# Attention scores by 32-row strips of the array instead of one masked 128-row product

## Chip, core and metric

The kernel runs on one core of a Trainium2 chip. The metric is the device time of one execution in microseconds (us). All data is float32. Engines are named as in the profile: PE is the matrix engine (PEld its weight loads), DVE the vector engine, ACT the scalar engine, POOL GpSimd, SP the engine that issues most DMAs. A "record" is one line of the profiler's own log: each float32 matmul leaves two weight-load records and two matmul records, each transpose by the identity one of each.

## What is computed

Four residual layers on x of shape (16, 256, 128), each on a layernorm of x:

```python
x = x + attn_a(ln(x))   # softmax in blocks of 64 tokens, 16 heads of 8
x = x + ffn(ln(x))      # top 2 of 8 experts, hidden 512, silu(g) * u
x = x + attn_b(ln(x))   # attention over the FIRST axis (16 positions), plus a bias
x = x + ffn(ln(x))      # same experts and weights

def attn_a(x):                       # b, block n, token i/j, head h, d = 8
    scores = einsum('bnihd,bnjhd->bnhij', q, k) / sqrt(8)
    return einsum('bnhij,bnjhd->bnihd', softmax(scores), v)
def attn_b(x):                       # sequence of 16, one per t of 256; same heads
    scores = einsum('bhqd,bhkd->bhqk', q / sqrt(8), k) + bias
    return einsum('bhqk,bhkd->bqhd', softmax(scores), v) @ out_w.T + out_b
```

## The kernel before

**Data and stages.** x lies in SBUF as four quarters `xq[q]` of 64 tokens, each 128 partitions by 8 groups by 128 channels. A group is two sequences of 64 tokens, so attention A has 32 groups of two blocks. Attention B has 32 groups of 128 tokens too, taken two at a time ("dg", 16 of them). Each quarter of attention is followed by `router`, which sorts token rows by expert into DRAM; `experts` then runs units of 256 or 128 rows.

**Order of work.** The main loop (L1199 to L1250) weaves generators: each `yield` is a step, and `weave` spreads steps of the router, of the next `prepare_a` or `begin_b` and of expert units between the steps of `attention_a` or `attention_b`. The counts BEGIN_A and BEGIN_B (L1190) tell `weave` how many steps a side has. From that the tile framework's scheduler makes one fixed order per engine when the kernel is built; each engine runs its order strictly in sequence and waits on semaphores. PSUM buffers are few: two for scores (`ps_sc`), two for all transposes, values and outputs (`ps_mm`, tag mm), three for `ps_gu`.

**Queries and keys.** `prepare_a` and `prepare_b` make, for half a quarter (512 tokens), the transposed q and k with channels on partitions: partition 32r + 8j + d holds head 4r + j, channel d. `keys` (L410) writes four copies of k by four ACT instructions in `four` (L388, recorded at L391); copy j keeps only the channels of the heads with index j in each strip of 32 partitions and is zero elsewhere (mask K_HM). `queries` (L404) also writes four copies: copy r keeps only the strip of partitions 32r to 32r + 31 (`q_scale`, `q_bias`, built at L371 to L380).

**Scores.** With those zeros a full 128-row product gives the right heads. In `attention_a` (L473), for each block b of a group, two matmuls (L487) with 128 stationary columns (two copies r by 64 tokens) and 256 moving columns (four copies j by 64 tokens) fill the bank `sc` of that block. In `attention_b` (L563), four matmuls per group (L593) with 128 stationary columns (four copies r by 32 tokens) and 128 moving ones fill one bank.

**After the scores.** In A, DVE takes the row maxima `mx` (L495) and writes sc - mx to `ex` (L496), ACT takes the exponential (L500), PE transposes `ex` (L506, `t_A`), ACT copies that to `eT` (L510), and 16 small matmuls with 64 stationary columns (L517, `o_A`) make the output, which `divided` (L442) normalises. B is the same with the bias added first (L600, `sb`) and outputs from 16 matmuls of 32 stationary columns (L630, `o_B`).

Of the kernel before, what the change touches and what calls it, by code (L numbers as in the profile page):

```python
# [114 lines left out]
def hybrid_kernel(  # L115
# [169 lines left out]
    def psum(name):  # L285
        return ps_mm.tile([P, 512], F32, tag="mm", name=name)
# [80 lines left out]
        nc.gpsimd.tensor_tensor(xs, xs, row.unsqueeze(1).to_broadcast([P, 4, C]), ALU.add)  # L367

    q_scale = const.tile([P, 4], F32, name="q_scale")  # L371
    q_bias, k_bias = {}, {}
    for r in range(4):
        nc.vector.tensor_reduce(
            q_scale[:, r : r + 1], k_sb[:, K_ID + 32 * r : K_ID + 32 * (r + 1)], AX.X, ALU.max
        )
    nc.vector.tensor_scalar(q_scale, q_scale, SCALE, None, ALU.mult)
    for col in (B_Q, B_IQ):
        q_bias[col] = const.tile([P, 4], F32, name=f"q_bias{col}")
        nc.vector.tensor_scalar(q_bias[col], q_scale, b_sb[:, col : col + 1], None, ALU.mult)  # L380
    for col in (B_K, B_IK):
        k_bias[col] = const.tile([P, 4], F32, name=f"k_bias{col}")
        nc.vector.tensor_scalar(
# [15 lines left out]
    def product(src, w, name):  # L399
        p = ps_gu.tile([P, CH], F32, tag="gu", name=name)  # L400
        nc.tensor.matmul(p, lhsT=w, rhs=src, start=True, stop=True)
        return p

    def queries(qT, src, w, col, name):  # L404
        yield from four(
            lambda r, p: (qT[:, :, r, :], p.rearrange("p (a k) -> p a k", k=qT.shape[3])),
            product(src, w, f"q_{name}"), q_scale, q_bias[col],
        )

    def keys(kx, src, w, col, name):  # L410
        yield from four(
# [47 lines left out]
    def prepare_a(q, half):  # L459
        n = f"A{q}_{half}"  # L460
        lnT = p2.tile([P, CH // BS, 2, BS], F32, tag="src", name=f"lnT_{n}")
        qT = p2.tile([P, CH // BS, 4, BS], F32, tag="qT", name=f"q_{n}")
        kx = p2.tile([P, 4, CH], F32, tag="kx", name=f"k_{n}")

        def put(_, pt):
            nc.scalar.copy(*spread(lnT, pt, 2))

        yield from layernorm_t(q, [half], n, put)
        yield from keys(kx, lnT[:, :, 0], wk_sb, B_K, n)
        ready[q, half] = lnT, qT, kx  # L470
        yield from queries(qT, lnT[:, :, 0], wq_sb, B_Q, n)

    def attention_a(q, half):  # L473
        lnT, qT, kx = ready.pop((q, half))
        for g in range(4 * half, 4 * half + 4):
            n = f"A{q}_{g}"
            vt = va[g % 2]
            values(vt, lnT, g % 4, 2, wv_sb, n)
            yield


            ex = p2.tile([P, 2, 8, BS], F32, tag="ex", name=f"ex_{n}")
            for b in range(2):
                sc = ps_sc.tile([P, 512], F32, tag="sc", name=f"sc_{n}_{b}")
                blk = 2 * (g % 4) + b
                for v in range(2):
                    nc.tensor.matmul(  # L487
                        sc[:, v * 4 * BS : (v + 1) * 4 * BS],
                        lhsT=qT[:, blk, 2 * v : 2 * v + 2, :].rearrange("p r k -> p (r k)"),
                        rhs=kx[:, :, blk * BS : (blk + 1) * BS],  # L490
                        start=True, stop=True,
                    )
                sc3 = sc.rearrange("p (h k) -> p h k", k=BS)
                mx = p3.tile([P, 16], F32, tag="mx", name=f"mx_{n}_{b}")
                nc.vector.tensor_reduce(mx[:, 0:8], sc3, AX.X, ALU.max)  # L495
                beat[0] = nc.vector.tensor_tensor(  # L496
                    ex[:, b], sc3, mx[:, 0:8].unsqueeze(2).to_broadcast([P, 8, BS]),
                    ALU.subtract,
                ).ins
                turn_of[0] = nc.scalar.activation(ex[:, b], ex[:, b], AF.Exp).ins  # L500
                yield
            eT = p2.tile([P, 2, 4, P], F32, tag="eT", name=f"eT_{n}")
            for b in range(2):
                pt = psum(f"t_{n}_{b}")
                for i in range(4):
                    nc.tensor.transpose(  # L506
                        pt[:, i * P : (i + 1) * P],
                        ex[:, b, 2 * i : 2 * i + 2, :].rearrange("p h k -> p (h k)"), ident,
                    )
                turn_of[0] = nc.scalar.copy(eT[:, b].rearrange("p a b -> p (a b)"), pt).ins  # L510
                yield
            po = psum(f"o_{n}")
            for b in range(2):
                for i in range(8):

                    u, v = i // 2 % 2, i // 4
                    nc.tensor.matmul(  # L517
                        po[b * BS : (b + 1) * BS, i * 18 : (i + 1) * 18],
                        lhsT=eT[:, b, 2 * v + i % 2, u * BS : (u + 1) * BS],
                        rhs=vt[:, b, 2 * i : 2 * i + 2, :].rearrange("p h d -> p (h d)"),  # L520
                        start=True, stop=True,
                    )
            att = divided(po[:, 0 : H * (D + 1)], n)
            beat[0] = att_last[0]
            if g == 4 * half:
                add_row(q, half, bv_bc)
            nc.gpsimd.tensor_tensor(xq[q][:, g, :], xq[q][:, g, :], att, ALU.add)  # L527
            yield
# [15 lines left out]
    def prepare_b(q, half):  # L544
        n = f"B{q}_{half}"
        xt = p2.tile([P, CH // 32, 4, 32], F32, tag="src", name=f"xt_{n}")
        qT = p2.tile([P, CH // 32, 4, 32], F32, tag="qT", name=f"q_{n}")
        kx = p2.tile([P, 4, CH], F32, tag="kx", name=f"k_{n}")
        px = psum(f"xt_{n}")
        nc.tensor.matmul(  # L550
            px, lhsT=wt_sb, rhs=ready[q][:, half * CH : (half + 1) * CH], start=True, stop=True
        )
        nc.scalar.activation(  # L553
            *spread(xt, px, 4), AF.Identity, bias=b_sb[:, B_TOR : B_TOR + 1]
        )
        yield
        yield from keys(kx, xt[:, :, 0], wi_sb[:, P : 2 * P], B_IK, n)
        ready[q, half] = xt, qT, kx
        yield from queries(qT, xt[:, :, 0], wi_sb[:, 0:P], B_IQ, n)
# [3 lines left out]
    def attention_b(q, half):  # L563
# [15 lines left out]
        for dg in range(2 * half, 2 * half + 2):  # L579
# [3 lines left out]
                yield  # L583


            ex = p2.tile([P, 2, H, 32], F32, tag="ex", name=f"ex_B{q}_{dg}")
            for gg in range(2):
                g = 2 * dg + gg
                n = f"B{q}_{dg}_{gg}"
                sc = ps_sc.tile([P, 512], F32, tag="sc", name=f"sc_{n}")  # L590
                for j in range(4):
                    blk = 4 * (g % 4) + j
                    nc.tensor.matmul(  # L593
                        sc[:, j * P : (j + 1) * P],
                        lhsT=qT[:, blk].rearrange("p r k -> p (r k)"),
                        rhs=kx[:, :, blk * 32 : (blk + 1) * 32],
                        start=True, stop=True,
                    )
                sb = p2.tile([P, H, 32], F32, tag="sb", name=f"sb_{n}")
                nc.vector.tensor_tensor(  # L600
                    sb, sc.rearrange("p (h k) -> p h k", k=32),
                    pair_bias.unsqueeze(1).to_broadcast([P, H, 32]), ALU.add,
                )
                yield
                mx = p3.tile([P, 16], F32, tag="mx", name=f"mx_{n}")
                nc.vector.tensor_reduce(mx, sb, AX.X, ALU.max)
                beat[0] = nc.vector.tensor_tensor(
                    ex[:, gg], sb, mx.unsqueeze(2).to_broadcast([P, H, 32]), ALU.subtract
                ).ins
                turn_of[0] = nc.scalar.activation(ex[:, gg], ex[:, gg], AF.Exp).ins  # L610
                yield
            for gg in range(2):
# [15 lines left out]
                for j in range(4):  # L628
                    for r in range(4):
                        nc.tensor.matmul(  # L630
                            po[32 * j : 32 * (j + 1), r * 36 : (r + 1) * 36],
                            lhsT=eT[:, 0, j, 32 * r : 32 * (r + 1)],
                            rhs=vb[gg][:, j, 4 * r : 4 * r + 4, :].rearrange(
                                "p h d -> p (h d)"
                            ),
                            start=True, stop=True,
                        )
# [549 lines left out]
        yield from normal_b(q)  # L1187
        yield from prepare_b(q, 0)

    BEGIN_A, BEGIN_B = 3 + 4, 5 + 10 + 5  # L1190
    ALONE = 8

    FIRST = BEGIN[0] + ALONE
# [5 lines left out]
    for layer in range(2):  # L1199
# [10 lines left out]
        for hq in range(2 * NQ):  # L1210
# [15 lines left out]
            else:  # L1226
                main = attention_b(q, half)
                if half == 0:
                    sides.append((prepare_b(q, 1), 5, 0, 3 * n // 4))
                elif q < NQ - 2:  # L1230
                    sides.append((begin_b(q + 1), BEGIN_B, 0, 4 * n // 5))
                wanted, goal = (0, GOAL[hq]) if q < NQ - 1 else (1, OWN[hq])
# [59 lines left out]
```

## Time and profile before

| what | value |
|---|---|
| runs, us | 1013.77 median of 3 (1010.72 to 1017.89) |
| profiled execution, us | 964.67 |
| its span from first to last instruction, us | 962.9 |
| granted PE clock, mean over the span | 0.943 |
| PE busy | 836.8 us (87%) |
| PEld busy | 715.1 us (74%) |
| DVE busy | 554.3 us (58%) |
| ACT busy | 482.1 us (50%) |
| POOL busy | 336.5 us (35%) |
| attention A, scores: first to last matmul | 18.0 to 282.4 us |
| attention B, scores: first to last matmul | 468.4 to 730.8 us |
| score matmul records A, B | 256 of 426 ns, 256 of 285 ns (mean) |

Durations come from the profiled execution, which was about 5% shorter than the runs. The end of a matmul is modelled by the profiler and contains the emptying of the array, so records of neighbouring matmuls overlap; the spacing of starts tells what a matmul costs in a sequence.

### The profile page before, as it was taken

To read this page: it belongs to the slowest core of one execution; us is meant where nothing else is said; L and a number is where in the kernel's file an instruction comes from. 1 tells how busy PE (TensorE), PEld (TensorE's weight loads), DVE (VectorE), ACT (ScalarE), POOL (GpSimd) and SP (SyncE) were. 2 spreads that over 40 slices of the span, in tenths; PEclk is the share of its full clock that TensorE was granted. 3 is DMA by queue.
4 is the path that set the end of the run, shared out by engine and by line. 5 is a ranking of instruction groups with operands and counts; after the bars stand their busy time and mean duration, and the time that the engine had idled before them with its cause. 6 is when DMAs were issued, how large, how long until landed. Compare 5 with 4: busy or idle time off the path is not lost.

```text
span 962.9 us, 18911 instructions
## 1 busy us (share of the span) xinstructions
PE 836.8 (87%) x6684; PEld 715.1 (74%) x6684; DVE 554.3 (58%) x1653; ACT 482.1 (50%) x1029; POOL 336.5 (35%) x381
## 2 busy tenths in 40 slices
PE   4999798979999989996978768996888899899993
PEld 2777676768888779995856656895577787799983
DVE  2666665654856944544673664684369478444563
ACT  4667366357345434444744746742664433344441
POOL 2112360532355563332000162162224537433321
PEclk9999999799999999997997989998999899999997
DMA  7800000043215538995400021317310443699994
GB/s 164 255 20 1 18 29 1 29 140 137 89 65 181 185 99 319 306 325 192 142 23 1 1 79 46 115 47 257 122 45 29 150 144 121 231 326 310 351 386 112
DMA packets 67006, 134.71 MB, mean 140 GB/s; under 512 B 9088, under 2 KB 46720, under 8 KB 66912
## 3 DMA queue, kind: packets, MB, share of 16 engines
q1 hardware_dynamic: 56400, 114.70, 35.9%
q0 software_dynamic: 8640, 17.97, 5.4%
q8 instruction: 53, 0.87, 0.4%
q10 hardware_dynamic: 1872, 0.83, 0.4%
q14 instruction: 41, 0.34, 0.1%
HBM read 112.33 MB, written 27.43 MB: 145 GB/s over the span
## 4 chain that ended last, share of the span: by engine, by line
PE 37%; DVE 9%; ACT 8%; DMA 5%; issue 3%; POOL 1%; SPq 1%; POOLq 0%; DVEq 0%; ACTq 0%
PE u L1057 8%; PE g L1057 8%; PE acc L995 7%; PE v_B L428 3%; DMA xin<-sorted_in 2%; PE o_B L630 2%; PE sc_B L593 2%; DMA w<-w_all 2%; ACT ln_B L345 1%; ACT k_B L391 1%; ACT xt_B L553 1%; PE y L1013 1%; DVE th L1071 1%; DVE h L1073 1%; ACT q_B L391 1%
## 5 line engine op out<-in xcount | busy, mean ns | idle before, releaser
L1023 POOL DMA_INDIRECT results<-yo,to x142 | 139.5, 983 | 259.4 <-ACT yo L1019 225.8
L1071 DVE SCALAR_TENSOR_TENSOR th<-th,g 128x512 f32<-128x512 f32 x142 | 96.8, 681 | 117.0 <-ACT th L1070 116.4
L1057 PE MATMUL u<-xT,w 128*128 128x128 f32 (+1 forms) x864 | 155.5, 318 | 8.0 <-DVE th L1071 7.9
L1057 PE MATMUL g<-xT,w 128*128 128x128 f32 (+1 forms) x864 | 154.7, 315 | 8.4 <-DMA w<-w_all 5.5
L995 PE MATMUL acc<-h,w 128*128 128x128 f32 (+1 forms) x864 | 153.0, 314 | 4.1 <-DVE h L1073 4.1
L780 POOL DMA_INDIRECT sorted_in<-rows,pos_i_F x128 | 124.9, 976 | 79.7 <-issue 28.7
L1070 ACT ACTIVATE th<-g 128x512 f32<-128x512 f32 x142 | 84.9, 598 | 116.0 <-PE g L1057 112.2
L1057 PEld LDWEIGHTS g<-xT,w 128*128 128x128 f32 x864 | 124.2, 194 | 20.4 <-issue 7.2
L1057 PEld LDWEIGHTS u<-xT,w 128*128 128x128 f32 x864 | 124.8, 198 | 17.1 <-DVE th L1071 11.4
L995 PEld LDWEIGHTS acc<-h,w 128*128 128x128 f32 x864 | 123.6, 195 | 12.5 <-DVE h L1073 6.4
L1073 DVE TENSOR_TENSOR h<-th,u 128x512 f32<-128x512 f32 x142 | 97.3, 685 | 16.3 <-PE u L1057 6.7
L487 PE MATMUL sc_A<-k_A,q_A 128*128 128x256 f32 x256 | 78.5, 426 | 18.5 <-DVE ex_A L496 13.8
L517 PEld LDWEIGHTS o_A<-va,eT_A 128*64 128x64 f32 x1024 | 61.1, 141 | 15.5 <-ACT eT_A L510 6.3
L487 PEld LDWEIGHTS sc_A<-k_A,q_A 128*128 128x128 f32 x256 | 47.2, 208 | 29.2 <-issue 8.6
L1003 ACT COPY yT<-acc 128x128 f32<-128x128 f32 (+1 forms) x108 | 32.3, 299 | 69.1 <-PE acc L995 67.8
L517 PE MATMUL o_A<-va,eT_A 128*64 128x18 f32 x1024 | 65.7, 215 | 0.8 <-ACT eT_A L510 0.7
L988 ACT COPY xT<-xt 128x128 f32<-128x128 f32 (+1 forms) x108 | 32.3, 299 | 60.4 <-PE xt L986 57.5
L495 DVE TENSOR_REDUCE mx_A<-sc_A 128x8 f32<-128x512 f32 x64 | 43.4, 679 | 29.0 <-PE sc_A L487 29.0
L510 ACT COPY eT_A<-t_A 128x512 f32<-128x512 f32 x64 | 36.1, 588 | 42.2 <-PE t_A L506 41.9
L1019 ACT ACTIVATE yo<-y,xin 128x128 f32<-128x128 f32 x142 | 48.0, 364 | 13.2 <-PE y L1013 13.2
L527 POOL TENSOR_TENSOR xq<-xq,att_A 128x128 f32<-128x128 f32 x32 | 14.6, 456 | 111.0 <-DVE att_A L447 76.6
L500 ACT ACTIVATE ex_A<-ex_A 128x512 f32<-128x512 f32 x64 | 39.9, 636 | 26.6 <-DVE ex_A L496 26.5
(181 smaller groups left out, 1349.4 us busy)
## 6 DMA issues: line engine op xcount, KB each, us to landing
w<-w_all SPq DMA_DIRECT2D x108, 768.0 KB
back<-results SPq DMA_DIRECT2D x14, 512.0 KB
xin<-sorted_in SPq DMA_DIRECT2D x74, 66.0 KB
xin<-sorted_in SPq DMA_DIRECT2D x34, 132.0 KB
results<-yo,to POOLq DMA_INDIRECT x142, 3.9
w_all<-in_wg SPq DMA_DIRECT2D x1, 2048.0 KB
w_all<-in_wu SPq DMA_DIRECT2D x1, 2048.0 KB
w_all<-in_wd SPq DMA_DIRECT2D x4, 512.0 KB
```

The source lines that it names most:

```text
L487: nc.tensor.matmul(sc[:, v * 4 * BS : (v + 1) * 4 * BS], lhsT=qT[:, blk, 2 * v : 2 * v + 2, :].rearrange("p r k -> p (r k)"), rhs=kx[:, :, ...
L495: nc.vector.tensor_reduce(mx[:, 0:8], sc3, AX.X, ALU.max)
L500: turn_of[0] = nc.scalar.activation(ex[:, b], ex[:, b], AF.Exp).ins
L517: nc.tensor.matmul(po[b * BS : (b + 1) * BS, i * 18 : (i + 1) * 18], lhsT=eT[:, b, 2 * v + i % 2, u * BS : (u + 1) * BS], rhs=vt[:, b, 2 * ...
L780: put_row = nc.gpsimd.indirect_dma_start(out=sorted_in[layer], out_offset=bass.IndirectOffsetOnAxis(ap=pos_i[:, k, g : g + 1], axis=0), in ...
L995: nc.tensor.matmul(acc[:, 0:size], lhsT=w[:, 2, hc * P : (hc + 1) * P], rhs=h[:, j * size : (j + 1) * size], start=(hc == 0), stop=(hc == ...
L1019: nc.scalar.activation(y[:, b, :], py[:, b * P : (b + 1) * P], AF.Identity, scale=t[:, b, C : C + 1],)
L1023: put_row = nc.gpsimd.indirect_dma_start(out=results[layer], out_offset=bass.IndirectOffsetOnAxis(ap=to[:, b : b + 1], axis=0), in_=y[:, b ...
L1057: nc.tensor.matmul(p[:, j * size : (j + 1) * size], lhsT=w[:, k, hc * P : (hc + 1) * P], rhs=xT[:, 0:size], start=True, stop=True,)
L1070: turn_of[0] = nc.scalar.activation(th, pg, AF.Tanh, scale=0.5).ins
L1071: nc.vector.scalar_tensor_tensor(th, th, 1.0, pg, ALU.add, ALU.mult)
L1073: beat[0] = nc.vector.tensor_tensor(h, th, pu, ALU.mult).ins
```

## The change

The query is written once, unmasked, by one ACT instruction: `qT` becomes 128 partitions by 512 tokens. Each score product is split by strip r: stationary operand `qT[32r:32r+32, block]`, moving operand the same 32 partitions of the four key copies. The result of strip r goes to its own output partitions.

- A: eight matmuls per group (32 rows, 64 stationary columns, 256 moving) in place of four. A bank now holds strips 2v and 2v + 1 of both blocks, where it held both halves of one block; the loops after it run over v, and `o_A` picks its operands accordingly. Both banks are allocated ahead of all eight matmuls.
- B: 32 matmuls per pair of groups (32 rows, 32 stationary columns, 128 moving) in place of eight, j outermost, then the group gg, then r. Strip r of group gg lands on output partitions 32((r + gg) mod 4); `o_B` reads it back from there. Both banks are allocated ahead.
- `queries` has one step less, so BEGIN_A, BEGIN_B and the count for `prepare_b` fall by one.

```diff
-    q_scale = const.tile([P, 4], F32, name="q_scale")
     q_bias, k_bias = {}, {}
-    for r in range(4):
-        nc.vector.tensor_reduce(
-            q_scale[:, r : r + 1], k_sb[:, K_ID + 32 * r : K_ID + 32 * (r + 1)], AX.X, ALU.max
-        )
-    nc.vector.tensor_scalar(q_scale, q_scale, SCALE, None, ALU.mult)
     for col in (B_Q, B_IQ):
-        q_bias[col] = const.tile([P, 4], F32, name=f"q_bias{col}")
-        nc.vector.tensor_scalar(q_bias[col], q_scale, b_sb[:, col : col + 1], None, ALU.mult)
+        q_bias[col] = const.tile([P, 1], F32, name=f"q_bias{col}")
+        nc.vector.tensor_scalar(q_bias[col], b_sb[:, col : col + 1], SCALE, None, ALU.mult)
...
     def queries(qT, src, w, col, name):
-        yield from four(
-            lambda r, p: (qT[:, :, r, :], p.rearrange("p (a k) -> p a k", k=qT.shape[3])),
-            product(src, w, f"q_{name}"), q_scale, q_bias[col],
-        )
+        behind_act(
+            nc.scalar.activation(
+                qT, product(src, w, f"q_{name}"), AF.Identity, bias=q_bias[col], scale=SCALE
+            )
+        )
+        yield
...
+            scs = [
+                ps_sc.tile([P, 512], F32, tag="sc", name=f"sc_{n}_{v}") for v in range(2)
+            ]
             for b in range(2):
-                sc = ps_sc.tile([P, 512], F32, tag="sc", name=f"sc_{n}_{b}")
                 blk = 2 * (g % 4) + b
-                for v in range(2):
+                of_blk = slice(blk * BS, (blk + 1) * BS)
+                for r in range(4):
+                    of_r = slice(32 * r, 32 * (r + 1))
                     nc.tensor.matmul(
-                        sc[:, v * 4 * BS : (v + 1) * 4 * BS],
-                        lhsT=qT[:, blk, 2 * v : 2 * v + 2, :].rearrange("p r k -> p (r k)"),
-                        rhs=kx[:, :, blk * BS : (blk + 1) * BS],
-                        start=True, stop=True,
+                        scs[r // 2][
+                            r % 2 * BS : (r % 2 + 1) * BS, b * 4 * BS : (b + 1) * 4 * BS
+                        ],
+                        lhsT=qT[of_r, of_blk], rhs=kx[of_r, :, of_blk], start=True, stop=True,
                     )
...
+            for j in range(4):
+                for gg in range(2):
+                    blk = 4 * ((2 * dg + gg) % 4) + j
+                    of_blk = slice(blk * 32, (blk + 1) * 32)
+                    for r in range(4):
+                        of_r = slice(32 * r, 32 * (r + 1))
+                        to = (r + gg) % 4 * 32
+                        nc.tensor.matmul(
+                            scs[gg][to : to + 32, j * P : (j + 1) * P],
+                            lhsT=qT[of_r, of_blk], rhs=kx[of_r, :, of_blk],
+                            start=True, stop=True,
+                        )
...
-    BEGIN_A, BEGIN_B = 3 + 4, 5 + 10 + 5
+    BEGIN_A, BEGIN_B = 3 + 3, 5 + 10 + 4
```

## The prediction

> **What bounds the kernel now.** I read the busy shares first, then the stages, then the timeline around the scores, then the chain of work that ended last.
>
> ```profile
> PE 836.8 (87%) x6684; PEld 715.1 (74%) x6684; DVE 554.3 (58%) x1653; ACT 482.1 (50%) x1029; POOL 336.5 (35%) x381
> PEclk9999999799999999997997989998999899999997
> ```
>
> PE has the most work at nearly full clock; no other engine is above 58%. Busy time by stage says whether that holds where the change is (columns: stretch, length, then busy PE, PEld, DVE, ACT, POOL with their records, clock, DMA share, GB/s):
>
> ```profile
> 70.00:120.00 50.00, 42.89 (x351) 34.16 (x350) 30.23 (x105) 27.11 (x54) 15.61 (x18) 0.93 0.03 9
> 230.00:292.00 62.00, 60.65 (x454) 51.63 (x453) 40.70 (x126) 26.82 (x55) 26.87 (x31) 0.97 0.22 72
> 475.00:600.00 125.00, 96.78 (x999) 77.67 (x996) 71.60 (x241) 68.96 (x122) 26.69 (x27) 0.88 0.11 33
> ```
>
> Attention A (18 to 292 us) has PE busy for 249 of 274 us over its stretches; attention B (460 to 760) for 250 of 300, and much less at 475 to 600, where it waits. PE's waits at the scores are short: 13.8 us in all for DVE's `ex` (the bank is still being read), 6.8 us for ACT's `q_A`. From 352 us on the chain of waits is complete, and has the four query copies in a row once per quarter:
>
> ```profile
> 464.08 2.11 ACT q_B L391 x3
> 515.87 2.68 ACT q_B L391 x4
> 585.56 2.68 ACT q_B L391 x4
> 696.03 2.11 ACT q_B L391 x3
> ```
>
> So PE's own stream counts in both stages, discounted where it waits, and a shorter query step counts in B.
>
> **The change part by part.**
>
> *1. Price of a score product now.* In a stream PE pays starts, not durations.
>
> ```profile
> 468.38 1.06 PE L593 MATMUL sc_B<-k_B,q_B 128*128 128x128 f32 x8
> 491.86 0.92 PE L630 MATMUL o_B<-vb,eT_B 128*32 128x36 f32 x32 [0.96 <-ACT eT_B L623]
> 492.71 0.55 PE L617 MATMUL t_B<-k_sb,ex_B 128*128 128x128 f32 x3
> 70.06 0.38 PE L487 MATMUL sc_A<-k_A,q_A 128*128 128x256 f32 x1
> 70.37 1.83 PE L517 MATMUL o_A<-va,eT_A 128*64 128x18 f32 x32
> ```
>
> Eight sc_B records take 1.06 us; less the last one's 0.275 that is 0.112 us each, taken below as 0.107 for 128 columns and 0.213 for 256 (proportional to columns). A: 128 matmuls x 2 x 0.213 = 54.7 us. B: 128 x 2 x 0.107 = 27.3 us. Together 82 us.
>
> *2. Do products of different strips run together?* One after the other the new ones cost more: A 256 x 0.427 = 109 us, B 512 x 0.213 = 109 us, 136 us more. The nearest row is `o_B`: its 32 records go to four output strips, eight to each. By proportion 36 columns cost 0.030 us, serially 0.97 us for all; the trace has 32 in 0.92 with a last one of 0.20, so (0.92 - 0.20) / 31 = 0.023 us apart. Single starts tell why: the strips begin at 491.861, 492.019, 492.176 and 492.334, each strip keeps its own pace of 0.032 us, and the second strip starts before records six to eight of the first (492.045, 492.078, 492.110). So strips of output columns do overlap here, and records enter at 0.158 / 8 = 0.020 us, 0.040 per matmul. That is output strips alone; strips of input rows occur nowhere in this trace. The Trainium skill, "TensorE: Matmul & The Clock Gate", Part 3, says they overlap too, but that matmuls start strictly in program order. By that rule the second record of a strip holds up all behind it: in unbroken runs A would take 9 x 0.213 = 1.92 us a group (1.71 before), B 33 x 0.107 = 3.5 us a pair (1.71), together 6.8 + 29 = 36 us more. By the row (starts out of order) it is what follows under 3. I take the row, and keep the rule as a rival.
>
> *3. The order in which they are issued.* The built order of PE's instructions breaks the scores up. Of A's 256 matmuls 26 stand alone, 14 runs have two, 19 three, 13 four, 14 more: 86 runs with other work between. B's 512 stand in 43 runs, seven alone. With 0.040 us per entry and each strip serial (0.427 us a matmul in A, 0.213 in B) I add up each run to its slowest strip: A 55.9 us, B 28.3, together 84.2 against 82.0. The overlap only pays for the split. If every group were one run, A would take 0.97 a group, 31 us.
>
> *4. Changes of tile size.* The last sc_A record starts at 70.06, and streams 0.213; `o_A` starts 0.31 after it, so 0.094 is lost. `o_B` to `t_B` gives 0.129 - 0.032 = 0.097. The built orders hold 156 such changes before and 369 after: 213 more, some 140 in A and 73 in B. At 0.094: 13.2 and 6.9 us.
>
> *5. Lookahead.* Before, the first score bank of an A group was finished ahead of the previous group's first transpose in 27 of 31 cases; after, in 10 of 31, and in 8 not even ahead of its outputs. DVE then starts `mx` and `ex` (0.679 each) later, and behind it wait exp on ACT, the transposes and `o_A`. 17 groups x up to 1.36 = 23 us; below nothing it cannot fall. I take a third, 8 us, since two groups are in flight. In B the first bank is ready after 27 x 0.040 + 0.213 = 1.3 us where it was 0.85: 16 x 0.45 = 7 us, half of it exposed, 3 us.
>
> *6. Query copies.* ACT issues one instruction in place of four, 0.67 us apart (2.68 / 4): 2.0 x 16 = 32 us less on an engine that is busy for half the time. Their writing is contiguous now, which I price as before. On the chain in B stand (0.15 + 2.11) + 2.68 + 2.68 + (2.11 + 0.15) = 9.9 us, and 9.9 - 4 x 0.67 = 7.2 us go. In A `q_A` was waited for 6.8 us; I take 4 off. The setup's DVE instructions go at nothing: DVE waits for the first load of x then, and uncovered they'd be under 2 us.
>
> *Sum.* PE's extra stream is exposed by some 0.6 (between 0.3, if it falls into its waits, and 1). A: (1.3 + 13.2) x 0.6 + 8 - 4 = +12.7. B: (1.0 + 6.9) x 0.6 + 3 - 7.2 = +0.5. Together +13 on 964.7 us. The runs' median is 1.05 times that execution; scaled alike +14, so 1028 us.
>
> Nothing is added for DVE, POOL or the queues: row counts and shapes on DVE stay the same, and SP's transfers keep their order.
>
> **The rivals.**
>
> *ACT's relief decides: faster.* Place: ACT's FIFO, where exponentials and `eT` copies stand behind query copies. For it: the chain rows above, and waits of the outputs on `eT_A` (7.0 us). Against it: ACT is at 50%, and PE's added stream follows the same loop. Price: my sum has 11 of the 32 us come through; the time falls below that of before from 13 + 11 = 24 on; at all 32 the sum is 13 + 11 - 32 = -8, and with the PE stream mostly hidden (exposure 0.3) -15: 999 us.
>
> *Strips overlap only in part.* By the program-order rule +36 us, or, if two row strips cannot write to one bank together (the Trainium skill, "TensorEngine Tiling (Array Packing)", Gotcha 1, unqualified as to partitions; no run here shows it), B's four strips of a bank go in turn: 16 x 3.4 - 27 = +27. With the changes of size, 36 + 20 = 56, exposed by 0.7 (lookahead 11 and relief 11 cancel): about +40, 1055 us. `o_B` speaks against it.
>
> *No overlap of row strips (the change does not do what it says).* +136 + 20 us on PE, 0.75 exposed: +118, 1135 us.
>
> **How the numbers follow.** Small loss 0.47, own range 1008 to 1048; ACT's relief 0.23, 985 to 1006; partial overlap 0.18, 1040 to 1080; none 0.12. From low to high 990 to 1080 leaves out the last and a little of the second. A measurement of this kernel tells about 1% (10 us). Faster by over 1%: 0.22 of the relief's 0.23. Within 1% (1003.6 to 1023.9): 0.19 of the small loss and 0.01 of the relief, 0.20. Slower: 0.28 + 0.18 + 0.12 = 0.58.
>
> **What would show it.** Starts of one strip's records 0.213 us (A) and 0.107 (B) apart with other strips' between them: step 2. About 0.1 us between stream end and next start in 213 new places: step 4. A longer wait of `mx_A` for `sc_A` (29.0 us now): step 5. `q_A` and `q_B` with 16 instructions each and fewer than 3 us on the chain: step 6. The forecast is wrong if the granted clock in 18 to 292 us falls under 0.9, if score records are spaced serially, or if PE waits so long anyway that 20 us of changes vanish.

## The result and the profile after

The changed kernel takes 1108.17 us (median of 4, 1097.42 to 1117.24) against 1013.99 (1010.72 to 1017.89): 1.089 times before, 95% interval 1.080 to 1.098. Ratios and intervals leave out a kernel's slow runs, those over 1.5% above its fastest (here the one of 1117.24). The forecast was 1028 us with a range of 990 to 1080, so it is wrong in size; the direction is right.

The chips on which these kernels ran differ: the kernel before takes 965 to 966 us on some, 1014 to 1023 us on others. Each run's time is therefore given as a ratio to the kernel before on the same chip. Profiles could not be paired like that: the profile of before is from a chip of the first kind (965 us), the first profile of the change from one of the second.

The page of the changed kernel, span, busy shares and granted clock, the rows shown of before:

```profile
span 1095.6 us, 20904 instructions
PE 950.1 (87%) x7708; PEld 748.2 (68%) x7708; DVE 558.9 (51%) x1648; ACT 453.7 (41%) x981; POOL 336.0 (31%) x381
PEclk9557656555688999899979797899799899899997
```

PE's share is 87% as before, ACT has lost the 28 us of query copies, DVE has hardly moved. The third row is new: attention A lies in slices 1 to 15, and in slices 2 to 11 the array gets 5 to 7 tenths of its clock where it had 7 to 9. The busy times per stretch for 200 to 300 us, before and then after (columns: stretch, length, busy PE, PEld, DVE, ACT, POOL with their records, then the clock):

```profile
200.00:300.00 100.00, 94.10 (x680) 79.01 (x679) 60.86 (x201) 49.54 (x103) 39.92 (x47) 0.97 0.35 117
```
```profile
200.00:300.00 100.00, 96.58 (x539) 63.46 (x540) 41.33 (x144) 34.82 (x64) 27.13 (x32) 0.55 0.04 13
```

PE is busy nearly all the time in both, and gets through 539 records where it got through 680; DVE and ACT are busy for about a third less. PE hardly waits; it is slow. Stage A, from the first score record to the last output record, goes from 270.0 to 375.7 us, 106 of the 133 us between the two spans:

```profile
18.00:288.00 270.00, 245.41 (x1960) 199.50 (x1960) 161.98 (x524) 154.32 (x286) 93.44 (x111) 0.95 0.24 75
```
```profile
17.30:393.00 375.70, 353.83 (x2217) 240.76 (x2218) 165.21 (x524) 141.56 (x263) 93.31 (x111) 0.66 0.18 55
```

Length times clock is 258 before (0.954) and 248 after (0.659): counted at full clock, the stage has become no longer. The mean is a share of time, for the profile's clock is either 1 or 0.5. In stage A it fell to half 6 times before and 7 times after; the longest such stretch was 10 us before and is 102 us after:

```profile
182.40:284.70 102.30, 98.71 (x512) 64.80 (x511) 39.95 (x147) 33.12 (x62) 22.30 (x27) 0.50 0.03 8
```

In the chain of waits of the changed kernel PE has 66%, and the score line leads.

```profile
PE 66%; DVE 10%; ACT 7%; issue 6%; DMA 5%; another core or an unknown queue 2%; POOL 2%; SPq 1%; POOLq 0%; DVEq 0%; ACTq 0%
PE sc_A L487 10%; PE g L1067 9%; PE u L1067 9%; PE acc L1005 8%; PE o_A L518 7%; PE t_A L507 4%; PE v_A L423 3%; PE v_B L423 2%; PE o_B L640 2%; PE y L1023 2%; PE lg_F L687 2%; DMA w<-w_all 2%; PE sc_B L600 1%; DMA xin<-sorted_in 1%
```

The strips do run together. The timeline of PE at four products of A in a row (eight records, at half clock), and at one pair of groups of B:

```profile
73.99 1.97 PE L487 MATMUL sc_A<-k_A,q_A 32*64 32x256 f32 x8
```
```profile
578.65 1.15 PE L600 MATMUL sc_B<-k_B,q_B 32*32 32x128 f32 x64
```

The eight records of A take 1.97 us; serially, at half clock, they would take 8 x 0.427 = 3.4. The 64 records of B take 1.15 us; serially they would take 64 x 0.107 = 6.8. The first starts are 0.007 us apart across eight tiles (four row strips, each with two output strips); within one tile they are 0.11 us apart.

### The profile page after: what moved, and what is told of

It is laid out like the page before. It is cut to its first block, busy times and chain, and to the rows that moved or that the text cites. A ratio compares the mean times of both kernels' runs of the same rounds, so it can differ in the third digit from the quotient of the medians.

```text
span 1095.6 us, 20904 instructions
## 1 busy us (share of the span) xinstructions
PE 950.1 (87%) x7708; PEld 748.2 (68%) x7708; DVE 558.9 (51%) x1648; ACT 453.7 (41%) x981; POOL 336.0 (31%) x381
## 4 chain that ended last, share of the span: by engine, by line
PE 66%; DVE 10%; ACT 7%; issue 6%; DMA 5%; another core or an unknown queue 2%; POOL 2%; SPq 1%; POOLq 0%; DVEq 0%; ACTq 0%
PE sc_A L487 10%; PE g L1067 9%; PE u L1067 9%; PE acc L1005 8%; PE o_A L518 7%; PE t_A L507 4%; PE v_A L423 3%; PE v_B L423 2%; PE o_B L640 2%; PE y L1023 2%; PE lg_F L687 2%; DMA w<-w_all 2%; PE sc_B L600 1%; DMA xin<-sorted_in 1%
## 5 line engine op out<-in xcount | busy, mean ns | idle before, releaser
L487 PE MATMUL sc_A<-k_A,q_A 32*64 32x256 f32 x512 | 116.3, 570 | 15.9 <-DVE ex_A L497 9.8
L518 PEld LDWEIGHTS o_A<-va,eT_A 128*64 128x64 f32 x1024 | 81.2, 185 | 30.9 <-issue 16.7
L518 PE MATMUL o_A<-va,eT_A 128*64 128x18 f32 x1024 | 87.2, 247 | 2.8 <-issue 2.0
L496 DVE TENSOR_REDUCE mx_A<-sc_A 128x8 f32<-128x512 f32 x64 | 43.6, 689 | 85.4 <-PE sc_A L487 81.3
L487 PEld LDWEIGHTS sc_A<-k_A,q_A 32*64 32x64 f32 x512 | 39.9, 183 | 47.9 <-issue 39.8
L507 PEld LDWEIGHTS t_A<-k_sb,ex_A 128*128 128x128 f32 x256 | 42.7, 192 | 23.5 <-issue 13.5
```

The source lines that it names most:

```text
L487: nc.tensor.matmul(scs[r // 2][r % 2 * BS : (r % 2 + 1) * BS, b * 4 * BS : (b + 1) * 4 * BS], lhsT=qT[of_r, of_blk], rhs=kx[of_r, :, of_bl ...
L507: nc.tensor.transpose(pt[:, i * P : (i + 1) * P], ex[:, v, 2 * i : 2 * i + 2, :].rearrange("p h k -> p (h k)"), ident,)
L518: nc.tensor.matmul(po[b * BS : (b + 1) * BS, i * 18 : (i + 1) * 18], lhsT=eT[:, v, 2 * b + i % 2, u * BS : (u + 1) * BS], rhs=vt[:, b, 2 * ...
```

## Experiments

Theory T, formed from these rows: the granted clock falls because products on strips of 32 rows do not keep it up; everything on PE in stage A then runs slower, whatever its own shape. Its form T1 says that the part of the array in use counts, its form T2 that only the time in which anything streams counts. The rival R, from the prediction's own terms: the 140 further changes of tile size in stage A and the lost lookahead set the time, and the clock only follows. The table has stage A of each run (first score record to last output record, clock averaged over it); the text gives the edits. Expectations in us are for a chip on which before takes 1014 us; the runs with A or B alone, `filled` and `switches` came to one with 966, so their ratios are to be compared.

| run | times before (95%) | stage A, us | clock | product |
|---|---|---|---|---|
| before | 1 | 270.0 | 0.954 | 258 |
| the change | 1.089 (1.080 to 1.098) | 375.7 | 0.659 | 248 |
| the change again | 1.080 (1.074 to 1.086) | 371.4 | 0.678 | 252 |
| a_only | 1.100 (1.096 to 1.103) | 362.3 | 0.675 | 245 |
| b_only | 0.995 (0.992 to 0.998) | 269.1 | 0.955 | 257 |
| filled | 1.057 (1.051 to 1.062) | 329.9 | 0.917 | 303 |
| half_filled | 1.058 (1.050 to 1.066) | 337.6 | 0.823 | 278 |
| switches | 1.030 (1.024 to 1.036) | 301.7 | 0.891 | 269 |
| tiny_rows128 | 1.029 (1.024 to 1.034) | 297.9 | 0.913 | 272 |
| cols64 | 1.011 (1.005 to 1.016) | 280.6 | 0.976 | 274 |
| cols32_one | 0.993 (0.987 to 0.999) | 280.0 | 0.967 | 271 |
| rows64 | 1.065 (two runs of four) | 337.0 | 0.727 | 245 |
| rows32 | 1.114 (1.107 to 1.121) | 394.4 | 0.597 | 235 |
| rows32_cols64 | 1.127 (1.120 to 1.134) | 394.0 | 0.62 (estimate, see there) | 243 |
| unsplit | 1.039 (1.032 to 1.045) | 316.7 | 0.768 | 243 |
| dense_turned | 1.024 (1.017 to 1.030) | 320.6 | 0.846 | 271 |

### One attention at a time

Attention A's new `prepare_a`, `attention_a` and single query copy in the kernel before, and attention B's likewise; the other one keeps its four query copies.

```diff
-        yield from queries(qT, lnT[:, :, 0], wq_sb, B_Q, n)
+        yield from queries1(qT, lnT[:, :, 0], wq_sb, B_Q, n)   # a_only: one copy
...
-        yield from queries(qT, xt[:, :, 0], wi_sb[:, 0:P], B_IQ, n)
+        yield from queries1(qT, xt[:, :, 0], wi_sb[:, 0:P], B_IQ, n)   # b_only
```

> Attention A's scores in strips, attention B as before. Theory T (the granted clock of the matrix engine falls to about a half because strips of 32 rows and 64 columns occupy little of the array): nearly all of the 94 us, 1090 to 1110 us, clock near 0.6 in stage A (18 to about 390 us) and as before behind it. Rival R (the 140 further changes of tile size in stage A and the lost lookahead set the time, the clock only follows from idle time): also slow, but with B's 73 changes missing at least 20 us less than the full change, under 1085.

> Attention B's scores in strips, attention A as before. T: B's scores are a small share of its stage, which is woven with dense expert products, so the clock hardly moves there: 1000 to 1025 us. R: 73 changes of 140 + 73, a third of the loss: 1035 to 1050 us.

A alone is 1.100 times before, just over T's 1.075 to 1.095 and far over R's 1.07; B alone is 0.995, in T's band. The whole loss is A's. R would have had B's 73 changes cost a third of it; they cost nothing that shows. Stage A of a_only, then the two stages of b_only (A, B), then stage B of before:

```profile
17.50:379.80 362.30, 343.47 (x2217) 234.05 (x2217) 165.29 (x524) 141.84 (x263) 93.54 (x111) 0.67 0.18 56
18.10:287.20 269.10, 244.25 (x1961) 198.24 (x1961) 161.94 (x524) 154.33 (x286) 93.41 (x111) 0.95 0.25 75
465.30:741.10 275.80, 227.29 (x3050) 174.93 (x3050) 172.80 (x566) 140.25 (x270) 81.07 (x81) 0.93 0.23 76
468.00:751.00 283.00, 232.90 (x2276) 191.98 (x2277) 173.12 (x568) 153.20 (x291) 79.67 (x81) 0.92 0.22 75
```

B's stage has 0.93 of the clock (0.92 before) and is 7.2 us shorter than the 283.0 of before. On chips of that kind stage B takes 282 to 287 us in the eight profiles with B as before and 276 to 280 in the three with B in strips (b_only, filled, unsplit). b_only is the fastest kernel on its chip, 0.5% under before (0.992 to 0.998).

### Added work that nobody reads

```diff
+            extra = ps_gu.tile([P, 512], F32, tag="gu", name=f"extra_{n}")
+            for b in range(2):
+                blk = 2 * (g % 4) + b
+                for v in range(2):          # half_filled: range(1)
+                    nc.tensor.matmul(
+                        extra[:, v * 4 * BS : (v + 1) * 4 * BS], lhsT=wk_sb,
+                        rhs=kx[:, :, blk * BS : (blk + 1) * BS], start=True, stop=True,
+                    )
```

> The full change, and in each group of attention A four dense products of 128 by 128 by 256 that nobody reads (54.7 us of added work at full clock). T: the clock in stage A comes back above 0.85 and the kernel gets FASTER by the added work, 1030 to 1075 us. R: the added work stands on top, with 24 more changes of tile size: 1140 to 1170 us, clock in stage A little changed in what it is worth.

> The full change with two unread dense products per group of attention A instead of four (27 us of added work at full clock). T1: the clock lies between 0.66 and 0.92, and the time below the full change's in spite of the added work, 1.04 to 1.075 times before (four products: 1.057). R: above the full change, 1.10 or more.

The full change with 54.7 us of useless dense products is 1.057 times before, in T's band (1.016 to 1.060), and faster than without them (1.080 and 1.089). Its clock row and its stage A:

```profile
PEclk9789999968899999999889897999889999999997
```
```profile
18.20:348.20 330.00, 322.77 (x2470) 231.57 (x2470) 163.21 (x524) 140.89 (x263) 93.31 (x111) 0.92 0.20 62
```

Stage A is 46 us shorter than with the change (32 shorter than in a_only, on the same chip) with 55 us more to do, at a clock of 0.92 and not 0.66. R predicted the opposite sign and falls. Half the filling brings 0.82 and the same time, 1.058: less added work, less clock. On its chip the change itself took 1.080.

### Which property of the product lowers the clock

Four versions of the kernel before, differing from it in the shape of attention A's score products, with the loop, the query copies and the banks of before. The two with 64 stationary columns need eight products per group in place of four; cols32_one also keeps `ex` in two fixed buffers, in attention B too. Those on 32 rows, and cols32_one, leave out part of the scores.

```diff
-                        lhsT=qT[:, blk, 2 * v : 2 * v + 2, :].rearrange("p r k -> p (r k)"),
-                        rhs=kx[:, :, blk * BS : (blk + 1) * BS],
# cols64, for r in range(4), to sc[r % 2 * BS : (r % 2 + 1) * BS, ...]:
+                        lhsT=qT[:, blk, r, :], rhs=kx[:, :, blk * BS : (blk + 1) * BS],
# rows32_cols64, the same with
+                        lhsT=qT[0:32, blk, 0, :], rhs=kx[0:32, :, blk * BS : (blk + 1) * BS],
# rows32
+                        lhsT=lnT[0:32, g % 4 * 2 + b].rearrange("p r k -> p (r k)"),
+                        rhs=kx[0:32, :, blk * BS : (blk + 1) * BS],
# cols32_one: stationary columns [:, 0:32] alone, to sc[0:32, ...]; mx, ex and exp on 32 partitions
```

> The kernel before, with attention A's dense score products cut in two along the output only: 128 rows by 64 stationary columns, two output strips in turn, all else as before (184 changes of tile size in stage A; before 92, full change 232). Streaming work and occupied array are those of before. T1 (the clock follows the occupied part of the array) and T2 (it follows the time in which anything streams): both clock above 0.85 in stage A, 1.01 to 1.04 times before, like the tiny products. R (changes of tile size): 92 of 140, 1.06 or more.

> As the 128 rows by 64 columns version, but on rows 0 to 31 alone (222 changes of tile size in stage A). It leaves out heads 4 to 15 and takes the first strip's scores for all. Same number of products, columns and moving elements as that version, two output strips in turn, a quarter of its occupied array. T1: clock in stage A near the full change's 0.66, 1.07 to 1.12 times before. T2: like that version within 1%, 1.01 to 1.04.

> The kernel before, with attention A's score products on 32 rows instead of 128 and all 128 columns (198 changes of tile size in stage A). It leaves out heads 4 to 15 and takes the normalised tokens for queries, so the scores are others; number, length and order of products are about those of before. T1: a quarter of the array, the clock in stage A falls towards 0.6 to 0.75 and the time is 1.05 to 1.11 times before. T2: as much streaming as before, clock above 0.85, 1.01 to 1.04.

> The kernel before, with attention A's score products on all 128 rows but only 32 stationary columns, always the same output strip (209 changes of tile size in stage A). It leaves out three of four queries in each score bank; the softmax instructions run on 32 partitions at the same length. As many products and as much streaming as the version on 32 rows and 128 columns, and the same quarter of the array. T1 in the form 'occupied area counts': clock in stage A falls to about 0.6, 1.09 to 1.13 times before. T1 in the form 'rows count': clock above 0.85, 1.00 to 1.04.

Stage A of cols64 and of rows32_cols64, which differ in the rows alone (and so in the scores that they make):

```profile
17.30:297.90 280.60, 258.52 (x2217) 187.42 (x2218) 163.89 (x524) 155.87 (x287) 93.61 (x111) 0.98 0.24 73
```
```profile
17.40:411.40 394.00, 389.03 (x2217) 263.68 (x2217) 165.66 (x524) 157.17 (x287) 93.52 (x111) 0.71 0.17 52
```

The record counts are equal, and the stages are 113 us apart. The second row's 0.71 is too high: the profile has no clock record ahead of 89.4 us in that run and counts what is missing as full clock (elsewhere at most 6.4 us of the stage are missing):

```profile
17.40:89.40 72.00, 71.99 (x357) 44.20 (x358) 26.03 (x63) 27.52 (x47) 6.85 (x9) 1.00 0.43 115
```

There neighbouring transposes of 128 columns start 0.213 us apart; at full clock, as in before, they start 0.109 apart. With half clock for these 72 us the stage has 0.62, an estimate, and length times clock is 243 against 274: no more work, done at a lower clock. cols64 shows one thing more: each of its query copies is zero outside one strip of 32 rows, and yet the clock stays at 0.98, so rows count although their stationary values are zero. The second pair has a quarter of the array each, once as rows and once as columns (groups of one form: records, busy time, mean duration in ns, idle time before them; rows32, then cols32_one):

```profile
L487 PE MATMUL sc_A<-k_A,lnT_A 32*128 32x256 f32 x256 | 119.6, 607 | 3.2 <-DVE ex_A L496 2.1 <-ACT k_A L391 1.1
```
```profile
L492 PE MATMUL sc_A<-k_A,q_A 128*32 128x256 f32 x256 | 71.9, 392 | 10.2 <-DVE kept L503 5.8 <-DVE mv_F L317 1.5 <-ACT q_A L391 1.4
```

The same 256 records with the same 256 moving columns last 607 ns on 32 rows and 392 on 128, at clocks of 0.60 and 0.97, and the times are 1.114 and 0.993 of before. So it is the rows. The form of T in which the occupied area counts falls with cols32_one; streaming time alone falls with both 32-row versions. Three of these times lie just outside the bands that came nearest: 1.114 and 1.127 above T1's, 0.993 below that of "rows count".

The traces also show when the clock moves, which I found afterwards and tested by no run of its own. It changes in steps of 3.413 us. Estimate for each step the time in which products stream, from 0.107 us per 128 moving columns (twice that at half clock), weight each product by its rows over 128, and take the sum as a share of the step. Over the 16 traces, at half clock 325 of the 371 steps with a share of 0.7 or more were followed by full clock, and 2 of the 675 below. At full clock 315 of the 351 steps below 0.4 were followed by half clock, and 28 of the 3322 above. Without the weight, counting any streaming, 534 steps at half clock reach 0.7 and still only 325 lead to full clock. In stage A the change has 75 steps at half clock where before had 7, and 8 of them reach a share of 0.7: with few rows the clock, once it is down, seldom comes back.

### Changes of tile size and the number of rows

```diff
+                tiny = ps_gu.tile([P, 512], F32, tag="gu", name=f"tiny_{n}_{b}")
# behind each of the 128 dense products; tiny_rows128 has ":" for "0:32" in both operands
+                    nc.tensor.matmul(
+                        tiny[0:32, 8 * v : 8 * v + 8], lhsT=qT[0:32, blk, 0, 0:32],
+                        rhs=kx[0:32, 0, blk * BS : blk * BS + 8], start=True, stop=True,
+                    )
# rows64: the rows32 version with 0:64 for 0:32
```

> The kernel before, with a tiny product of 32 rows, 32 columns and 8 moving columns behind each of the 128 dense score products of attention A (nobody reads it): 85 more changes of tile size in stage A, 177 where before had 92 and the full change 232. T: 85 x 0.094 us and some 5 us of tiny products, partly hidden: 1018 to 1030 us, clock in stage A above 0.85. R: 85 of 140 changes bring 85/140 of stage A's loss of about 100 us: 1060 to 1080 us.

> The tiny products behind attention A's dense score products again (32 columns, 8 moving, unread), now on 128 rows instead of 32; the built order of the matrix engine is that of the 32-row ones, with the same 85 more changes of tile size. If few rows lower the clock: clock in stage A above 0.93, 1.00 to 1.02 times before. If the changes of tile size do: clock near 0.89 and 1.025 to 1.04 as with 32 rows.

> The kernel before with attention A's score products on 64 rows and 128 columns (leaves out heads 8 to 15 and takes the normalised tokens for queries), in the built order of the 32-row version, 198 changes of tile size in stage A. If the clock follows the share of rows in proportion: between 32 rows (1.114) and 128, 1.03 to 1.07 times before, clock 0.75 to 0.88. If there is a threshold: either as with 32 rows, 1.10 or more, or 1.00 to 1.025.

Both tiny versions cost 3%: for the 32-row one T gave 0.4 to 1.6% and R 4.5 to 6.5%, and neither has it. The rows of the tiny products do not matter. Of some 30 us in stage A, length times clock explains 11 and 14; the rest is a clock of 0.89 and 0.91 instead of 0.954. cols64 has 92 more changes of size than before and a clock of 0.976, so the changes as such do not do it. The clock falls 10 and 13 times in stage A, where before has 6, each time after a step with a share under 0.4; why there are more such steps stays open. With 64 rows the time is 1.065, in the band of proportion, and the clock 0.73, just under it. That does not rule out a threshold: the mean is a share of time at 1 and at 0.5, and the two shares above, 0.4 and 0.7, act like thresholds in each step.

### The order of the products

The loop is turned so that the next group's scores stand ahead of this group's transposes, and each product follows the one before it; in dense_turned the scores are the dense ones, with B in strips.

```diff
+            if g == 4 * half:
+                yield from scores(g)
+            if g + 1 < 4 * half + 4:
+                yield from scores(g + 1)
+            ex = exs.pop(g)
...
+    def inrow(product):
+        if row_of[0] is not None:
+            follow(product.ins, row_of)
+        row_of[0] = product.ins
```

> The full change with attention A's loop turned so that the eight score products of the next group stand ahead of this group's transposes, kept in one row with the transposes and outputs: 41 runs instead of 86, 159 changes of tile size in stage A instead of 232, lookahead back. Some 25 us of the matrix engine's own work go. T1 or T2: the clock stays at 0.5 to 0.7 in stage A, so most of the loss stays, 1.05 to 1.09 times before. R: more than half of the loss of 9% goes, 1.02 to 1.045.

> Attention B in strips, attention A's products dense as before, but in the turned loop of the 'unsplit' version (scores of the next group ahead of this group's transposes, 74 changes of tile size in stage A). T1: the clock stays above 0.93 in stage A, and what the turned loop does by itself shows: 0.98 to 1.01 times before; if it is below 0.99 it beats both kernels.

Both miss. Unsplit keeps 3.9% of loss where T wanted 5 to 9, with a clock of 0.77 and not under 0.7, and so lies in R's band. But length times clock is 243 where the change had 248, so nearly all of what it gains comes with the clock and not from less work on PE, of which some 25 us were expected to go. The turned loop with dense products is not a gain but 2.4% slower, at 0.85 where T1 wanted over 0.93: its clock falls 15 times in stage A, again after steps with a share under 0.4, so full rows alone do not hold the clock where PE streams too little. Seen side by side the strips cost 1.5% in the turned loop (1.039 against 1.024, on two chips) and 10% in the loop of before. A likely reason is that four strips of an unbroken group stream at once and take less time from the full-row products, while broken ones stream singly; that is argued from the 41 runs against 86, and was not tried by itself.

### The full change again

> The full change once more, on the chip of the other experiments. All theories: 1.08 to 1.10 times before; attention A in strips alone was 1.10 and attention B alone 0.995, so if the two add up, 1.085 to 1.105, with a clock near 0.66 in stage A.

1.080, at the edge of the first band and just under that of the sum. Stage A has 371 us at 0.68. Stage B takes 307 us at 0.87 here; in cols32_one, whose attention B is that of before but for the fixed `ex` buffers, on the same chip, it takes 312 at 0.87:

```profile
576.60:883.20 306.60, 242.72 (x3050) 187.40 (x3050) 173.80 (x566) 140.22 (x270) 81.92 (x82) 0.87 0.20 69
484.70:796.70 312.00, 244.58 (x2283) 200.60 (x2282) 173.23 (x568) 153.73 (x291) 81.86 (x83) 0.87 0.20 68
```

So the longer stage B of the changed kernel's first profile (303 us) goes with the kind of chip and not with the change.

## Why the prediction was wrong

**Steps 1 and 3, the price of a stream, failed.** I took 0.107 and 0.213 us a record from the full-clock trace of before and kept them for a stage whose products the change itself alters. The term for A, (1.3 + 13.2) x 0.6 + 8 - 4 = +12.7 us, measured +92 us of stage A in a_only (362.3 - 270.0). Not the amount of work was wrong: at full clock stage A has 245 to 252 us with the change and 258 without. What failed is the clock at which it is done, 0.66 instead of 0.95: the 258 us of before at 0.659 would alone be 391 us, and the stage took 376. I named a clock under 0.9 as what would refute the forecast, and gave it neither price nor chance.

**A rule read too simply.** The Trainium skill, "TensorE: Matmul & The Clock Gate", Part 1, ties the half rate to an idle array and the full rate to a busy one. The trace's 96.58 us of 100 at 0.55 does not fit that, if busy means what the profile's busy column means. Full rate would have been my forecast, and the measurement decides: the rows in use count too, as the steps of the clock show above.

**Step 2 was right.** Row strips overlap, and their records start out of program order, so the description of the kernel before goes too far where it has every engine run its order strictly in sequence. Both rivals that had strips held up (partial overlap, none) fell: the first eight records of a pair of B, four to each bank, start 0.007 us apart. The second rival's 1135 us lies nearer to the result than my 1028 by luck alone. The spacing of entries was mis-sized: 0.007 us, not 0.020.

**Step 4, 0.094 us a change of size:** cols64 has 92 more and is 1.0105 times before, 10 us (5 to 16), or 0.05 to 0.17 each if the changes are all of it; it also has twice as many score products, and no run here parts the two. Small in any case.

**Step 5, lookahead:** DVE's wait for scores of A rose as foretold, 29.0 to 81.3 us (before, the change, rows32; us in all, times, longest):

```profile
DVE mx_A L495 <- PE sc_A L487: 29.0, 19, 4.2
DVE mx_A L496 <- PE sc_A L487: 81.3, 41, 5.6
DVE mx_A L495 <- PE sc_A L487: 75.4, 38, 6.4
```

But rows32, with the loop of before and a clock of 0.60, has 75.4 us, so a slow clock brings nearly all of it without the lost lookahead. The rise was foretold for a reason that is not needed. The B half of this step (+3 us) and B's exposed stream (+4.7) did not appear.

**Step 6, the query copies, held.** On the chain of waits of the changed kernel stand

```profile
627.82 0.58 ACT q_B L399
702.50 0.59 ACT q_B L399
```

1.2 us where 9.9 stood (`q_A` and `q_B` have 8 instructions each now, 16 together, and not 16 each). B alone gains 7.2 us in its stage and 0.5% in time; the sum for B said +0.5 us, because of the stream and lookahead terms that did not appear. That the gain is ACT's relief fits, but was not tried apart from the strips; in A the clock drowns it.

## What to carry to other kernels

A change of the shape of matrix products changes the clock for everything else in the stage; look at which products keep the full rows in use before trading a padded dense product for strips, and give the clock a case of its own in the forecast. Strips were free in attention B, whose 64 records per pair take 1.15 us and stand among dense expert products, and dear in attention A; that the expert products hold the clock there is argued and was not tried. A dense product that computes blocks nobody reads can be the cheaper one.

## What the runs showed of the hardware

- Rows, not columns, weigh on the granted clock: 32 rows by 128 columns 0.60, 64 by 128 0.73, 128 by 128 0.95, 128 by 32 0.97 in the same stage. Rows whose stationary values are zero count too (cols64, 0.98).
- The clock was 1 or 0.5, in steps of 3.413 us. It came back from half after steps whose streaming, weighted by rows over 128, filled 0.7 or more, and fell after steps below 0.4 (estimated shares; 325 of 371 steps and 315 of 351).
- Useless dense products raised it from 0.66 to 0.92 and made the kernel faster by 2 to 3% (1.057 against 1.080 and 1.089; half as many, on the chip of the 1.080, 1.058).
- Eight tiles of 32 by 32, two to each row strip, ran together: 64 records in 1.15 us.
- The kernel before runs at 965 to 966 us on some chips and at 1014 to 1023 on others. Stage B, 276 to 287 us at 0.90 to 0.93 on the former, takes 303 to 317 at 0.83 to 0.89 on the latter, whichever attention B it has; why stays open.
